# The A12 part of the linear layer by one Strassen level, joined to acc by VectorE, and block sums of x in another order

## Chip, cores and metric

One Trainium2 chip, one of its cores. The metric is the time of the kernel on the device in microseconds (us); the lower the better. Everything is in fp32.

## The reference

```python
# x: (1024, 512); weight: (64, 512, 512); lin_w: (512, 512); lin_b: (512,)
out_lin = x @ lin_w.T + lin_b
xv = einsum('bf,efm->bem', x, weight)
zp = einsum('bf,efm->bem', square(x), square(weight))
y = out_lin + 0.5 * sum(square(xv) - zp, axis=1)
```

The sum over the 64 embeddings e can be drawn into the squared weights for `zp`, so that this needs one matrix product at the end. What remains is 64 products of (1024 x 512) by (512 x 512), their squares summed over e, and one more such product for the linear layer.

## The kernel before

x stands transposed on the chip, with the features on the 128 partitions. It is cut into four blocks A11, A12, A21, A22: r (first digit) is the half of the batch rows, kk (second digit) the half of the features. Each block has four quarters of 256 columns. All products are made by Strassen's algorithm, which gets a 2 by 2 block product from seven products of sums in place of eight; the 64 embeddings' products use two levels of it, so there are 49 products of sums. The outer level (numbers "1" to "7", the code's `i`) combines the blocks of x; the inner level (`o`) combines quarters. `xs` holds all 7 x 7 sums of x, `SLOT` tells where. Of these, "1", "2" and "4" are A11, A12 and A22 as loaded; A21 lies apart. `outer_x(i)` makes the outer sums "5", "6", "7" and "3" (in two parts: three quarters at once, 768 wide, and the fourth, 256 wide), `inner_x(i)` the four inner sums of block i (256 wide). These additions run on VectorE, for "7" and "3" on GpSimd.

The weights are taken four embeddings at a time (16 rounds `q`). GpSimd makes their sums: `outer_t` (L380, 1024 wide), and `inner_t` (L391 `tp`, L393 `t6`, L395 `t4`). A unit (`unit`) is one outer product for one of two column halves j: seven matmuls of 512 columns (L421) into three PSUM tags, x (two banks), v and y (three banks each), with ScalarE copying x to y after the first and VectorE or ScalarE reading the banks between matmuls that accumulate on (L444 to L467). The squares are added to `acc`.

`acc[r]` gathers twice the linear layer and the squares, for the batch half r; `acc_blk(r, b)` is one of its four blocks. The end of the kernel halves it and subtracts half of `zp`.

Before the units the linear layer is put into `acc`. For r = 0, `lin(kk)` multiplies with plain matmuls: eight of 512 columns for A11 (kk = 0) and eight for A12 (kk = 1), four accumulating banks, which `lin_out` (L226) then writes to `acc[0]`, doubled. For r = 1, `lin_p` (L271) does one Strassen level: products "1", "5", "6", "2", "7", "3", "4", each with four matmuls of 256 columns (two kk, two j). Their right-hand sides are the linear weights `lw_sb` or sums of them `LT`, which `lin_t` makes on GpSimd (L284 to L292). Their left-hand sides are quarters of A21 and A22, or sums that `a21_a22_sums` makes (L252): eight additions, seven on VectorE, the eighth, "3" of A22, on GpSimd. Between products, ScalarE copies the bank x to y (L328) or writes twice a bank to `s_lin` or `acc` (`twice`, L303), and VectorE joins twice a bank and a part of `s_lin` into `acc` (`lin_join`, L309).

The order of work is written by hand. `st.at(t, fn)` puts a function at a place t, and `Stream.run` calls them in order of t; the schedule is manual, so each engine executes its instructions in exactly this order, waiting by semaphores for what they need. t is thus a place in a queue and no time. Unit 1 of the first round begins at t = 0. Before it stand, for VectorE: inner sums of "1" (-29) and "2" (-22), the A21/A22 sums (-20), outer and inner "5" (-16), the two joins (-5.5, -3.5), outer and inner "6" (-3.4). For GpSimd: the sums of the linear weights (-30, -29), its one A21/A22 sum, the weight sums of unit 1 (-11.5), of outer "5" (-11), of unit 2 (-5), outer and inner "7" of x (-4.7).

Of the kernel before, what the change touches and what calls it, by code (L numbers as in the profile page):

```python
# [8 lines left out]
F32 = mybir.dt.float32  # L9
AF = mybir.ActivationFunctionType  # L10
ALU = mybir.AluOpType
# [17 lines left out]
def kernel(  # L29
# [31 lines left out]
    nc = tc.nc  # L61
    _, _, _, Q = x.shape
    E, F, M = weight.shape
    P = 128
    NK = F // P
    HM = M // 2
    BK = 2 * HM
# [3 lines left out]
    spool = ctx.enter_context(tc.tile_pool(name="spool", bufs=3))  # L71
    psum = ctx.enter_context(
        tc.tile_pool(name="psum", bufs=3, space=bass.MemoryType.PSUM)
    )
# [19 lines left out]
    def acc_blk(r, b):  # L94
        return acc[r][:, :, b // 2, ts(b % 2, HM)]

    def by_j(bank):
        return bank.rearrange("p (j c) -> p j c", j=2)
# [8 lines left out]
    def xsl(i, o):  # L107
        return xs[:, SLOT[i], SLOT[o], :]

    st = Stream()  # L110
# [5 lines left out]
    lw_sb = T6.rearrange("p u l m -> p (u l) m")  # L116
# [29 lines left out]
    def quarter(r, kk, n):  # L146

        w = slice(0, 3) if n is None else n
        for i, rk in BLOCK.items():
            if rk == (r, kk):  # L150
                return a21[i] if n == 3 else xs[:, SLOT[i], w, :]
        return A21[:, w, :]

    def outer_x(i, eng=nc.vector):
        if i in BLOCK:
            return []

        def put(n):
            w = slice(0, 3) if n is None else n

            def of(o):
                return a21[o] if n == 3 else xs[:, SLOT[o], w, :]

            def src(r, kk):
                return quarter(r, kk, n)

            if i == "5":
                eng.tensor_add(of(i), src(1, 0), src(1, 1))
            elif i == "6":
                eng.tensor_sub(of(i), of("5"), src(0, 0))  # L170
            elif i == "7":
                eng.tensor_sub(of(i), src(0, 0), src(1, 0))
            else:
                eng.tensor_sub(of(i), src(0, 1), of("6"))

        return [lambda: put(None), lambda: put(3)]

    def inner_x(i, eng=nc.vector):
        add, sub = eng.tensor_add, eng.tensor_sub
        return [  # L180
            lambda: add(xsl(i, "5"), a21[i], xsl(i, "4")),
            lambda: sub(xsl(i, "6"), xsl(i, "5"), xsl(i, "1")),
            lambda: sub(xsl(i, "7"), xsl(i, "1"), a21[i]),
            lambda: sub(xsl(i, "3"), xsl(i, "2"), xsl(i, "6")),
        ]
# [7 lines left out]
    LIN = {}  # L193
# [7 lines left out]
            ps = psum.tile([P, BK], F32, tag="y", name=f"y_spin{n}", bufs=3)  # L201
            nc.tensor.matmul(ps, zero[:, 0:P], zero, start=True, stop=True)

    def lin(kk):

        order = [(s, j, l) for s in range(2) for j in range(2) for l in range(2)]
        if kk == 0:
            order.sort(key=lambda o: o[2])
        for s, j, l in order:
            n = 2 * s + j  # L210
            if kk == 0 and l == 0:
                tag = "xxvy"[n]
                LIN[n] = psum.tile(
                    [P, M], F32, tag=tag, name=f"lin{n}", bufs=2 if tag == "x" else 3
                )
            nc.tensor.matmul(  # L216
                LIN[n],
                quarter(0, kk, (0, 1, 3, 2)[2 * s + l])[:, ts(j, P)],
                lw_sb[:, 2 * kk + l, :],
                start=(kk == 0 and l == 0),  # L220
                stop=(kk == 1 and l == 1),
            )

    def lin_out(n):
        s, j = n // 2, n % 2
        nc.scalar.activation(  # L226
            acc[0][:, j, s],
            LIN[n],
            AF.Copy,
            scale=2.0,  # L230
        )

    def lin_x(kk, o):
        if kk == 1:
            return xsl("4", o)
        return A21[:, SLOT[o]] if o in "124" else A21_SUMS[:, "5673".index(o)]
# [3 lines left out]
    def a21_a22_sums():  # L240
        def put(kk, o, eng):
            def of(o):
                return lin_x(kk, o)

            raw = a21["4"] if kk else A21[:, 3]
            fn, a, b = {
                "5": lambda: (eng.tensor_add, raw, of("4")),
                "6": lambda: (eng.tensor_sub, of("5"), of("1")),
                "7": lambda: (eng.tensor_sub, of("1"), raw),
                "3": lambda: (eng.tensor_sub, of("2"), of("6")),  # L250
            }[o]()
            fn(of(o), a, b)  # L252

        return [
            lambda o=o, kk=kk: put(kk, o, nc.gpsimd if o == "3" and kk else nc.vector)
            for o in "5673"
            for kk in range(2)
        ]

    def lin_p(o, bank, first):  # L260
        def fn():
            if o == "1":
                for n in "xvy":
                    LIN[n] = psum.tile(
                        [P, BK], F32, tag=n, name=f"{n}_lin", bufs=2 if n == "x" else 3
                    )
                s_lin = spool.tile([P, 2, BK], F32, tag="s", name="s_lin")
                LIN["s2"], LIN["s5"] = s_lin[:, 0], s_lin[:, 1]
            for kk in range(2):
                for j in range(2):  # L270
                    nc.tensor.matmul(  # L271
                        LIN[bank][:, ts(j, HM)],
                        lin_x(kk, o)[:, ts(j, P)],
                        lin_rhs(lw_sb[:, ts(kk, 2)], LT[kk], o),
                        start=(first and kk == 0 and j == 0),
                        stop=True,
                        skip_group_check=True,
                    )

        return fn  # L280

    def lin_t(t, b):

        nc.gpsimd.tensor_sub(  # L284
            t[:, 0:2, :],
            b[:, :, HM:M],
            b.rearrange("p l m -> p (l m)")[:, 0:M].rearrange(
                "p (u c) -> p u c", u=2
            ),
        )  # L290
        nc.gpsimd.tensor_sub(t[:, 2, :], b[:, 1, HM:M], t[:, 0, :])
        nc.gpsimd.tensor_sub(t[:, 3, :], b[:, 1, 0:HM], t[:, 2, :])  # L292

    def lin_rhs(b, t, o):
        if o in "123":
            l, u = {"1": (0, 0), "2": (1, 0), "3": (1, 1)}[o]
            return b[:, l, ts(u, HM)]
        return t[:, "5764".index(o)]

    def twice(bank, dst):  # L300
        def fn():
            o = by_j(LIN[dst]) if dst in ("s5", "s2") else acc_blk(1, dst)
            nc.scalar.activation(o, by_j(LIN[bank]), AF.Copy, scale=2.0)  # L303

        return fn

    def lin_join(bank, s, blk):
        def fn():
            nc.vector.scalar_tensor_tensor(  # L309
                acc_blk(1, blk),  # L310
                by_j(LIN[bank]),
                2.0,
                by_j(LIN[s]),
                ALU.mult,
                ALU.add,
            )

        return fn

    st.at(-40, spin)  # L320
    for kk in range(2):
        st.at(-30 + 8 * kk, lambda kk=kk: lin(kk))
        st.at(-30 + kk, lambda kk=kk: lin_t(LT[kk], lw_sb[:, ts(kk, 2)]))
    for n in range(4):
        st.at(-20 + 2 * n, lambda n=n: lin_out(n))
    for t, fn in (
        (-14, lin_p("1", "x", True)),
        (-13.5, lambda: nc.scalar.copy(LIN["y"], LIN["x"])),  # L328
        (-12, lin_p("5", "v", True)),
        (-11.5, twice("v", "s5")),  # L330
        (-10, lin_p("6", "y", False)),
        (-9.5, twice("y", "s2")),
        (-8, lin_p("2", "x", False)),
        (-7.5, twice("x", 0)),
        (-6, lin_p("7", "y", False)),
        (-5.5, lin_join("y", "s5", 3)),
        (-4, lin_p("3", "v", False)),
        (-3.5, lin_join("v", "s2", 1)),
        (-2, lin_p("4", "y", False)),
        (-1.5, twice("y", 2)),  # L340
    ):
        st.at(t, fn)

    bias = const.tile([P, M], F32, tag="bias", name="bias")

# [189 lines left out]
    for q in range(NQ):  # L535
# [29 lines left out]
        for k, n, r, times in (  # L565
# [5 lines left out]
            for j in range(2):  # L571
                t = g0 + 14 * k + 7 * j + 14.6
# [11 lines left out]
        st.at(-100, lambda kk=kk, v=v: load_w(0, kk, v))  # L584


    for sums, t in (
        (inner_x("1"), -29),
        (inner_x("2"), -22),
        (a21_a22_sums(), -20),  # L590
        (outer_x("5") + inner_x("5"), -16),
        (outer_x("6") + inner_x("6"), -3.4),
    ):
        for n, fn in enumerate(sums):
            st.at(t + 0.1 * n, fn)
    for i, t in (("7", -4.7), ("3", 36.9)):
        for n, fn in enumerate(outer_x(i, nc.gpsimd) + inner_x(i, nc.gpsimd)):
            st.at(t + 0.1 * n, fn)
# [233 lines left out]
```

## Time and profile before

| | |
|---|---|
| median of 3 runs | 1406.15 us (1405.92 to 1406.15) |
| profiled execution, its own time | 1405.72 us |
| its span (first to last instruction) | 1403.9 us |
| busy: TensorE, VectorE, ScalarE, GpSimd | 1399.7, 869.0, 620.9, 1257.8 us |
| granted TensorE clock | 1.000 |
| linear layer, r = 0, plain matmuls (L216) on the chain | 14.00 us from 4.44 |
| linear layer, r = 1, Strassen products (L271) on the chain | seven of 1.73 us, from 18.44 |
| first matmul of the units (L421) | at 30.36 us |

PE is TensorE, PEld its weight loads, DVE is VectorE, ACT ScalarE, POOL GpSimd, SP SyncE, whose queue issues most loads. A line of a timeline gives the start and the length in us, engine, line of the kernel, operation, output <- inputs by the program's tile names, shape, and in brackets the idle time before it with what released it. The tile name z stands for `ZT`, in which the A21 quarters, their sums and `LT` lie at the start; t stands for `T6`, which first holds `lw_sb`, and for other tiles named t. A fp32 matmul appears as two records, each with its own weight load.

### The profile page before, as it was taken

The numbers are of one execution on the slowest core, as the hardware profiler recorded it, in microseconds if no ns is written. First come the engines' busy times: TensorE is split into PE (matmuls) and PEld (weight loads), VectorE is DVE, ScalarE is ACT, GpSimd is POOL, SyncE is SP. The second block draws the span as 40 slices with busy tenths as digits, with TensorE's granted clock in tenths as the row PEclk, the third lists the DMA queues.
The fourth block names the chain that finished last, engine by engine and source line by source line (L and its number), as shares of the span: only waits on it lengthen the run. The fifth ranks groups of instructions, "written<-read, shape, count | busy, mean of one in ns | idle before, by whom it ended". The sixth has DMA issues, their size and how long they took to land.

```text
span 1403.9 us, 11169 instructions
## 1 busy us (share of the span) xinstructions
PE 1399.7 (100%) x3340; PEld 634.8 (45%) x3340; DVE 869.0 (62%) x1263; ACT 620.9 (44%) x825; POOL 1257.8 (90%) x816
## 2 busy tenths in 40 slices
PE   9999999999999999999999999999999999999999
PEld 5444444444444444444444444444444444444446
DVE  6665656656566665656656566565656656566565
ACT  3444353453535444353453535444353453435443
POOL 7989899998999989898998989989898998989984
PEclk9999999999999999999999999999999999999999
DMA  5299898999989989898999989889898999989975
GB/s 217 60 225 213 192 203 175 221 187 218 197 180 225 182 206 210 192 207 174 222 187 217 202 178 224 179 206 209 199 202 175 225 185 217 202 181 221 181 166 135
DMA packets 58108, 273.63 MB, mean 195 GB/s; under 512 B 5440, under 2 KB 8000, under 8 KB 41792
## 3 DMA queue, kind: packets, MB, share of 16 engines
q0 software_dynamic: 36432, 198.20, 72.0%
q1 hardware_dynamic: 21328, 74.19, 15.1%
q10 hardware_dynamic: 288, 0.52, 0.1%
q8 instruction: 27, 0.44, 0.1%
q14 instruction: 33, 0.27, 0.1%
HBM read 72.61 MB, written 2.10 MB: 53 GB/s over the span
## 4 chain that ended last, share of the span: by engine, by line
PE 99%; DMA 0%; DVE 0%; issue 0%
PE y L421 41%; PE v L421 27%; PE x L421 27%; PE lin L216 1%; PE y_last L659 1%; PE x_last L659 0%; PE v_last L659 0%; PE y_lin L271 0%; DMA t<-lin_wT 0%; PE v_lin L271 0%; PE x_lin L271 0%; PE end L722 0%; DVE z L732 0%
## 5 line engine op out<-in xcount | busy, mean ns | idle before, releaser
L421 PE MATMUL y<-t,xs 128*128 128x512 f32 x896 | 421.3, 592 | 0.0
L475 ACT COPY y<-x 128x512 f32<-128x512 f32 x224 | 127.7, 570 | 610.9 <-PE x L421 610.8
L467 DVE TENSOR_TENSOR z<-y,s 128x512 f32<-128x512 f32 x192 | 132.6, 691 | 242.9 <-PE y L421 242.9
L421 PEld LDWEIGHTS y<-t,xs 128*128 128x128 f32 x896 | 170.1, 190 | 214.2 <-issue 210.4
L497 ACT ACTIVATE z<-z 128x1024 f32<-128x1024 f32 x256 | 260.2, 1054 | 12.0 <-POOL z L472 9.4
L421 PE MATMUL x<-w,xs 128*128 128x512 f32 x512 | 248.4, 592 | 0.0
L421 PE MATMUL v<-tp,xs 128*128 128x512 f32 x448 | 228.8, 592 | 0.0
L421 PE MATMUL y<-tp,xs 128*128 128x512 f32 x448 | 228.8, 592 | 0.0
L506 POOL DMA_DIRECT2D acc<-z x190 | 212.9, 1151 | 15.1 <-DMA acc<-z 11.0
L391 POOL TENSOR_TENSOR tp<-w 128x1024 f32<-128x1024 f32 x64 | 174.9, 2734 | 23.8 <-PE y L421 22.6
L421 PE MATMUL x<-t,xs 128*128 128x512 f32 x384 | 188.3, 592 | 0.0
L472 POOL TENSOR_TENSOR z<-z,s 128x1024 f32<-128x1024 f32 x64 | 149.6, 2354 | 42.7 <-DVE s L467 42.7
L467 DVE TENSOR_TENSOR z<-v,s 128x512 f32<-128x512 f32 x192 | 132.6, 691 | 72.5 <-PE v L421 71.0
L458 DVE TENSOR_TENSOR z<-y,z 128x512 f32<-128x512 f32 x192 | 132.3, 689 | 57.9 <-PE y L421 57.9
L380 POOL TENSOR_TENSOR t<-w,t 128x1024 f32<-128x1024 f32 x64 | 164.2, 2728 | 0.0
L458 DVE TENSOR_TENSOR z<-x,z 128x512 f32<-128x512 f32 x192 | 132.1, 688 | 36.6 <-PE x L421 35.1
L421 PEld LDWEIGHTS x<-w,xs 128*128 128x128 f32 x512 | 97.3, 190 | 122.0 <-issue 121.0
L391 POOL TENSOR_TENSOR tp<-t 128x1024 f32<-128x1024 f32 x48 | 130.0, 2708 | 19.2 <-PE y L421 19.1
L421 PEld LDWEIGHTS v<-tp,xs 128*128 128x128 f32 x448 | 85.1, 190 | 107.1 <-issue 103.1
L421 PEld LDWEIGHTS y<-tp,xs 128*128 128x128 f32 x448 | 85.1, 190 | 106.7 <-issue 106.7
L421 PE MATMUL v<-w,xs 128*128 128x512 f32 x256 | 130.7, 592 | 0.0
L446 DVE TENSOR_TENSOR s<-v,z 128x512 f32<-128x512 f32 x160 | 110.5, 691 | 29.4 <-PE v L421 28.7
(114 smaller groups left out, 1475.7 us busy)
## 6 DMA issues: line engine op xcount, KB each, us to landing
w<-weight SPq DMA_DIRECT2D x64, 1024.0 KB, 13.4
acc<-z POOLq DMA_DIRECT2D x128, 512.0 KB, 8.2
w_sum<-w_sb POOLq DMA_DIRECT2D x63, 1024.0 KB, 9.3
acc<-z POOLq DMA_DIRECT2D x62, 1024.0 KB, 8.1
w<-x SPq DMA_DIRECT2D x2, 1024.0 KB, 8.0
out<-z SPq DMA_DIRECT2D x7, 256.0 KB, 2.3
xs<-x SPq DMA_DIRECT2D x2, 384.0 KB, 7.0
t<-lin_wT ACTq DMA_DIRECT2D x2, 256.0 KB, 4.0
```

The lines of the kernel that those rows point to most:

```text
L216: nc.tensor.matmul(LIN[n], quarter(0, kk, (0, 1, 3, 2)[2 * s + l])[:, ts(j, P)], lw_sb[:, 2 * kk + l, :], start=(kk == 0 and l == 0), stop ...
L380: nc.gpsimd.tensor_sub(OUTER[i][:, u], a[:, u], b[:, u])
L391: nc.gpsimd.tensor_sub(t, b[:, 1], b[:, :, 0])
L421: nc.tensor.matmul(d[bank], xsl(i, o)[:, ts(j, P)], operand_b(q, i, o), start=start, stop=True, skip_group_check=True,)
L446: nc.vector.tensor_add(o, d[bank], zblk(q, addend, j, b))
L458: nc.vector.tensor_add(zblk(q, dst, j, b), d[bank], zblk(q, addend, j, b))
L467: nc.vector.tensor_add(s if both else zblk(q, dst, j, b), d[bank], s)
L472: nc.gpsimd.tensor_add(place(q, n)[:, 1, j], place(q, src)[:, 1, j], d["s"])
L475: st.at(t0 + 0.5, lambda: nc.scalar.copy(d["y"], d["x"]))
L497: lambda u=u: nc.scalar.activation(z[:, u, j], z[:, u, j], AF.Square),
L506: nc.gpsimd.dma_start(o, z, accum_op=ALU.add)
L659: nc.tensor.matmul(ps[:, ts(j, HM)], last_x(i)[:, (0, 1, 3, 2)[2 * s + l], ts(j, P)], last_w(i)[:, l, :], start=(start and j == 0 and l == 0),
```

## The change

- `lin()` has only the eight plain matmuls for A11; `lin_out` follows at once and writes its four banks to `acc[0]`.
- A12 gets the seven Strassen products of `lin_p` with r = 0: two matmuls of 256 columns each, with the inner sums of "2" in `xs` as left-hand sides. ScalarE copies x to y after the first; after each of the six others VectorE executes one scalar_tensor_tensor (`lin_add`), which adds twice the bank to what `acc[0]` or `s_lin` holds. They stand from t = -21.5 to -15.25, one step apart. The second set, r = 1, keeps its places and operations.
- The A21/A22 sums are spread between these, in their old order: -21, -19.5, -18.5, -16.5, -15.5, -15, -14.9 and -14.8.
- Outer "5" and outer "6" of x come together at -14.5, and inner "6" and inner "5" together at -3.4.

```diff
--- before.py
+++ after.py
@@ -201,24 +201,22 @@
             ps = psum.tile([P, BK], F32, tag="y", name=f"y_spin{n}", bufs=3)
             nc.tensor.matmul(ps, zero[:, 0:P], zero, start=True, stop=True)
 
-    def lin(kk):
-
-        order = [(s, j, l) for s in range(2) for j in range(2) for l in range(2)]
-        if kk == 0:
-            order.sort(key=lambda o: o[2])
+    def lin():
+
+        order = [(s, j, l) for l in range(2) for s in range(2) for j in range(2)]
         for s, j, l in order:
             n = 2 * s + j
-            if kk == 0 and l == 0:
+            if l == 0:
                 tag = "xxvy"[n]
                 LIN[n] = psum.tile(
                     [P, M], F32, tag=tag, name=f"lin{n}", bufs=2 if tag == "x" else 3
                 )
             nc.tensor.matmul(
                 LIN[n],
-                quarter(0, kk, (0, 1, 3, 2)[2 * s + l])[:, ts(j, P)],
-                lw_sb[:, 2 * kk + l, :],
-                start=(kk == 0 and l == 0),
-                stop=(kk == 1 and l == 1),
+                quarter(0, 0, (0, 1, 3, 2)[2 * s + l])[:, ts(j, P)],
+                lw_sb[:, l, :],
+                start=(l == 0),
+                stop=(l == 1),
             )
 
     def lin_out(n):
@@ -230,7 +228,9 @@
             scale=2.0,
         )
 
-    def lin_x(kk, o):
+    def lin_x(kk, o, r=1):
+        if r == 0:
+            return xsl("2", o)
         if kk == 1:
             return xsl("4", o)
         return A21[:, SLOT[o]] if o in "124" else A21_SUMS[:, "5673".index(o)]
@@ -257,22 +257,23 @@
             for kk in range(2)
         ]
 
-    def lin_p(o, bank, first):
+    def lin_p(r, o, bank, first):
         def fn():
             if o == "1":
                 for n in "xvy":
-                    LIN[n] = psum.tile(
-                        [P, BK], F32, tag=n, name=f"{n}_lin", bufs=2 if n == "x" else 3
+                    LIN[r, n] = psum.tile(
+                        [P, BK], F32, tag=n, name=f"{n}_lin{r}", bufs=2 if n == "x" else 3
                     )
-                s_lin = spool.tile([P, 2, BK], F32, tag="s", name="s_lin")
-                LIN["s2"], LIN["s5"] = s_lin[:, 0], s_lin[:, 1]
-            for kk in range(2):
+                s_lin = spool.tile([P, 2, BK], F32, tag="s", name=f"s_lin{r}")
+                LIN[r, "s2"], LIN[r, "s5"] = s_lin[:, 0], s_lin[:, 1]
+            kks = range(2) if r else (1,)
+            for kk in kks:
                 for j in range(2):
                     nc.tensor.matmul(
-                        LIN[bank][:, ts(j, HM)],
-                        lin_x(kk, o)[:, ts(j, P)],
+                        LIN[r, bank][:, ts(j, HM)],
+                        lin_x(kk, o, r)[:, ts(j, P)],
                         lin_rhs(lw_sb[:, ts(kk, 2)], LT[kk], o),
-                        start=(first and kk == 0 and j == 0),
+                        start=(first and kk == kks[0] and j == 0),
                         stop=True,
                         skip_group_check=True,
                     )
@@ -299,47 +300,48 @@
 
     def twice(bank, dst):
         def fn():
-            o = by_j(LIN[dst]) if dst in ("s5", "s2") else acc_blk(1, dst)
-            nc.scalar.activation(o, by_j(LIN[bank]), AF.Copy, scale=2.0)
+            o = acc_blk(1, dst) if isinstance(dst, int) else by_j(LIN[1, dst])
+            nc.scalar.activation(o, by_j(LIN[1, bank]), AF.Copy, scale=2.0)
 
         return fn
 
-    def lin_join(bank, s, blk):
+    def lin_add(r, bank, addend, dst):
+
+
+        def of(n):
+            return acc_blk(r, n) if isinstance(n, int) else by_j(LIN[r, n])
+
         def fn():
             nc.vector.scalar_tensor_tensor(
-                acc_blk(1, blk),
-                by_j(LIN[bank]),
-                2.0,
-                by_j(LIN[s]),
-                ALU.mult,
-                ALU.add,
+                of(dst), by_j(LIN[r, bank]), 2.0, of(addend), ALU.mult, ALU.add
             )
 
         return fn
 
     st.at(-40, spin)
+    st.at(-30, lin)
     for kk in range(2):
-        st.at(-30 + 8 * kk, lambda kk=kk: lin(kk))
         st.at(-30 + kk, lambda kk=kk: lin_t(LT[kk], lw_sb[:, ts(kk, 2)]))
     for n in range(4):
-        st.at(-20 + 2 * n, lambda n=n: lin_out(n))
-    for t, fn in (
-        (-14, lin_p("1", "x", True)),
-        (-13.5, lambda: nc.scalar.copy(LIN["y"], LIN["x"])),
-        (-12, lin_p("5", "v", True)),
-        (-11.5, twice("v", "s5")),
-        (-10, lin_p("6", "y", False)),
-        (-9.5, twice("y", "s2")),
-        (-8, lin_p("2", "x", False)),
-        (-7.5, twice("x", 0)),
-        (-6, lin_p("7", "y", False)),
-        (-5.5, lin_join("y", "s5", 3)),
-        (-4, lin_p("3", "v", False)),
-        (-3.5, lin_join("v", "s2", 1)),
-        (-2, lin_p("4", "y", False)),
-        (-1.5, twice("y", 2)),
-    ):
-        st.at(t, fn)
+        st.at(-29 + 0.1 * n, lambda n=n: lin_out(n))
+    for r, t0, dt in ((0, -21.5, 1), (1, -14, 2)):
+
+        def copy_y(r=r):
+            nc.scalar.copy(LIN[r, "y"], LIN[r, "x"])
+
+        for n, (o, bank, first, fn) in enumerate(
+            (
+                ("1", "x", True, copy_y),
+                ("5", "v", True, twice("v", "s5") if r else lin_add(0, "v", 3, "s5")),
+                ("6", "y", False, twice("y", "s2") if r else lin_add(0, "y", 1, "s2")),
+                ("2", "x", False, twice("x", 0) if r else lin_add(0, "x", 0, 0)),
+                ("7", "y", False, lin_add(r, "y", "s5", 3)),
+                ("3", "v", False, lin_add(r, "v", "s2", 1)),
+                ("4", "y", False, twice("y", 2) if r else lin_add(0, "y", 2, 2)),
+            )
+        ):
+            st.at(t0 + dt * n, lin_p(r, o, bank, first))
+            st.at(t0 + dt * n + 0.25 * dt, fn)
 
     bias = const.tile([P, M], F32, tag="bias", name="bias")
 
@@ -584,15 +586,16 @@
         st.at(-100, lambda kk=kk, v=v: load_w(0, kk, v))
 
 
-    for sums, t in (
+    for sums, *times in (
         (inner_x("1"), -29),
         (inner_x("2"), -22),
-        (a21_a22_sums(), -20),
-        (outer_x("5") + inner_x("5"), -16),
-        (outer_x("6") + inner_x("6"), -3.4),
+        (a21_a22_sums(), -21, -19.5, -18.5, -16.5, -15.5, -15),
+        (outer_x("5") + outer_x("6"), -14.5),
+        (inner_x("6") + inner_x("5"), -3.4),
     ):
         for n, fn in enumerate(sums):
-            st.at(t + 0.1 * n, fn)
+            k = min(n, len(times) - 1)
+            st.at(times[k] + 0.1 * (n - k), fn)
     for i, t in (("7", -4.7), ("3", 36.9)):
         for n, fn in enumerate(outer_x(i, nc.gpsimd) + inner_x(i, nc.gpsimd)):
             st.at(t + 0.1 * n, fn)
```

## The prediction

> **What bounds the kernel now.** I read the page's first and fourth parts, then the chain of waits, then the timelines of TensorE (PE), VectorE (DVE), ScalarE (ACT) and GpSimd (POOL) over the first 45 us, the only place that the change touches. From the page, busy time by engine and shares of the chain:
>
> ```profile
> PE 1399.7 (100%) x3340; PEld 634.8 (45%) x3340; DVE 869.0 (62%) x1263; ACT 620.9 (44%) x825; POOL 1257.8 (90%) x816
> PE 99%; DMA 0%; DVE 0%; issue 0%
> ```
>
> PE carries 99% of the chain: a matmul fewer is gained one for one, a PE wait is lost one for one, and no slack elsewhere can give it back. From the chain in order of time (start, length):
>
> ```profile
> 4.44 14.00 PE lin L216 x32
> 18.44 1.73 PE x_lin L271 x8
> ...
> 28.80 1.73 PE y_lin L271 x8
> ```
>
> PE runs without a gap from 4.44. Matmul records come two to a matmul, so 32 records are 16 matmuls of the linear layer's upper half; then seven Strassen products of four 256-wide matmuls each, 1.73 us a product.
>
> Now the engines beside it, DVE first (start, length, tile, idle before):
>
> ```profile
> 12.66 0.41 DVE L252 TENSOR_TENSOR z<-z 128x256 f32<-128x256 f32 x1
> ...
> 17.19 2.47 DVE L182 TENSOR_TENSOR xs<-xs 128x256 f32<-128x256 f32 x1
> 19.58 1.48 DVE L183 TENSOR_TENSOR xs<-xs,z 128x256 f32<-128x256 f32 x1
> 20.99 1.49 DVE L184 TENSOR_TENSOR xs<-xs 128x256 f32<-128x256 f32 x1
> 27.19 0.69 DVE L309 SCALAR_TENSOR_TENSOR acc<-y_lin,s_lin 128x512 f32<-128x512 f32 x1 [4.72 <-PE y_lin L271]
> ```
> ```profile
> 14.16 2.72 POOL L252 TENSOR_TENSOR xs<-xs 128x256 f32<-128x256 f32 x1 [2.37 <-DVE xs L252]
> 16.84 2.54 POOL L391 TENSOR_TENSOR tp<-w 128x1024 f32<-128x1024 f32 x1
> 19.45 1.33 POOL L393 TENSOR_TENSOR t<-w,tp 128x512 f32<-128x512 f32 x1
> 20.86 1.33 POOL L395 TENSOR_TENSOR t<-w,t 128x512 f32<-128x512 f32 x1
> 22.15 4.85 POOL L380 TENSOR_TENSOR t<-w,w 128x1024 f32<-128x1024 f32 x2
> ```
>
> The same 256-wide block sum takes 0.41 us while POOL is idle and 1.48 to 2.47 us while POOL computes. The ends show why: POOL's L391 ends at 19.38 and DVE's L182 0.28 later; POOL's L393 ends at 20.78 and DVE's L183 0.28 later; L395 at 22.19 and L184 at 22.48. Each DVE sum sits out one whole POOL instruction, and POOL's next one, issued first, goes ahead of DVE's next. They alternate one for one. Before, this cost nothing: DVE was done at 22.48 and then idle 4.72 us until the first join at 27.19.
>
> **What the skill says.** The Trainium skill, "SBUF — State Buffer", section "Who interferes with whom", says that a VectorE instruction with two SBUF inputs contends with a GpSimd instruction that reads SBUF and the second to issue fully blocks, while one with at most one SBUF input doesn't contend. The trace agrees: the 2.47 us above, against 0.69 us for the join (one PSUM input) at 27.19, inside POOL's L391 of 26.96 to 29.31. "PSUM — Partial Sum Buffer", section "PSUM bank collisions raise a hardware error", wants PSUM guarded by semaphore per bank: a matmul into bank y waits until the reader of y is through. The trace shows one such hand-over with one product between: ACT's copy runs 31.42 to 31.99, and the next matmul but one starts at 33.07 instead of 32.94, 0.13 us late. "TensorE: Matmul & The Clock Gate", section "Part 1: The HAM clock gate", says that an idle window of about 3.4 us halves the PE clock. Here the spin matmuls at the start are 0.85 us apart per pass, later passes 0.43: agreed for a cold start; no idle stretch inside this run tests the rest.
>
> **The change, part by part.**
>
> 1. *Matmuls.* Eight of the 16 512-wide matmuls go: 8 x 0.858 = 6.87 us (in the PE timeline 21 matmuls from 39.11 to 57.14 take 18.03). Fourteen 256-wide ones come: 14 x 0.432 = 6.05 (28 take 12.09 from 18.27 to 30.36). Gain **0.82 us**. The order of the first eight and the DMA loads are unchanged, so they start at 4.44 as now.
>
> 2. *PSUM hand-overs in the new seven products*, which are 0.865 us apart where the old seven are 1.73. P1 would start at 11.41, P5 at 12.27. P6 needs ACT's copy of x to y, with one product between: 0.13 as in the first unit. P7 needs y after DVE has read it for s2, P4 needs y after DVE has read it for block 3, again one product between, and DVE's read is 0.69 against ACT's 0.57: 0.13 + 0.12, about 0.24 each. Sum **+0.61 us** (0.3 to 1.2). The four `lin_out` activations (0.60 each) are done by 12.2, ahead of their readers.
>
> 3. *DVE's new order.* Inner sums of x for "2" end at 12.7 as now. Then come, interleaved, the A21/A22 sums and seven joins of 0.69 that wait for PE (the old kernel had two). So sum 6 of A22, over at 14.08 now, runs behind the join of P7: P7 ends 16.10, join 16.30 to 16.99, sum at about 17.3. POOL's own sum (L252) waits for it and stands first in POOL's queue, ahead of the weight sums of unit 1: POOL starts them at 18.1 instead of 16.84, 1.3 us late. That alone costs nothing: their first use, unit 1's P5, is at 31.22.
>
> 4. *What is now behind what.* After sum 6, DVE still has seven two-SBUF sums before the second set's joins: A21's 7, A22's 7, A21's 3, outer 5 in two parts, outer 6 in two parts; outer 6 stood behind those joins until now. From 18.1 POOL has work without a gap. With holds from the rows above (POOL 2.23 for 1024 wide, 17.15 to 19.38; 1.12 for 512; DVE 0.28 for 256 wide, 0.81 for 768 wide, 30.66 to 31.47):
>  - A21's 7 behind L252: to 18.40.
>  - A22's 7 behind tp (18.40 to 20.63): to 20.91. The join of P4 goes in the gap.
>  - A21's 3 behind t6 (to 22.03): 22.31.
>  - outer 5 behind t4 (to 23.43): 24.24; its second part behind L380 (to 26.47): 26.75.
>  - outer 6 behind the second L380 (to 28.98): 29.79; its second part behind the tp of unit 2 (to 32.02): 32.30.
>
>  Then, and only then, the join of bank y of the second set: 32.24 to 32.93. P7 of that set is over at 26.71, and P4 accumulates onto the same bank. P4's turn is 28.44; with the hand-over (0.22) it starts at 33.15. **Stall 4.71 us.** Queued behind the join are the second join and the inner sums; behind P4 on PE is everything.
>
> 5. *The stretch after.* Inner 6 and inner 5, eight sums, replace outer 6 and inner 6, six sums (29.44 to 37.43 now). Alternating with POOL's t6, t4 and x7 sums they end at about 41.5. The units then begin at 34.88 and want their first join of y by about 41.8: no stall, and the 0.1 us that PE now loses at 38.15 goes. POOL's later weight sums are 2.6 us later, PE 4.5: their cover grows.
>
> ACT, SP and all DMAs keep their order; their work lies far from these waits, so I cost it at nothing.
>
> Sum: -0.82 + 0.61 + 4.71 - 0.1 = **+4.4 us**. The profiled execution has span 1403.9 and own time 1405.72; with 4.4, 1410.1. The median shown is 0.43 above that execution, so **1410.5**. A measurement of this kernel can tell about 0.2%, 2.8 us, from no change. The new order's stall is in no row of before. Its bounds: 0, if DVE gets through between POOL instructions; 4 to 5.2, if POOL's start moves by half a microsecond; and, as PE is idle over 3.4 us, a halved clock after it, which by the page's 3.4 us window and one or two such windows at half speed is an estimate of 1.7 to 3.4 more. I take no drop, because the window must fall within a gap only 1.3 us longer, and keep it for the range.
>
> **Rivals.**
> - *Clock drop* (0.24): the stall and 1.7 to 3.4 us more, up to 1413.9.
> - *DVE goes first* (0.18), the case on the other side: not slower. One row speaks for it: POOL's L252 at 14.16 takes 2.72 us, while DVE ran five sums back to back at full speed; POOL got in only when DVE paused at 16.3. If DVE's run of sums shuts POOL out so, outer 6 is done before 26.9 and P4 doesn't wait. Then only the eight inner sums from 29.2 count: nine microseconds of alternation to 38.3, the y join of unit 1 wanted by 36.6, a stall of 1.7 at most. Sum -0.82 + 0.61 + 1.6: 1407.5 (1406.3 to 1408). It decides if two of the four POOL instructions after 22.3 fall behind DVE. Against it: at 7.99, 19.58 and 35.62 a ready DVE sum stood behind POOL each time.
> - *All hidden* (0.11): just parts 1 and 2, 1405.3 to 1406.3; the same would be seen if the half of the layer didn't go to Strassen's form at all.
>
> **How the numbers follow.** Stall without clock drop 0.44, with it 0.24: slower 0.68. DVE first 0.18 and hidden 0.11 are within 0.2%: with a little rounding 0.29. Faster by 2.8 us needs more than the change removes from PE plus all of its waits now: 0.03. Range 1406.5 to 1413.6: it takes in the rival that isn't slower, and leaves out the hidden case, faster, and the top of the clock drop. The likeliest's own range is 1409.9 to 1411.2.
>
> **What would show it.** Right: 14 matmuls of 256 between 11.4 and about 18; POOL's L252 near 17.4; a PE gap of about 4.7 us before the second set's P4, released by DVE, whose outer 6 sums (L170) end next to 32 at 2 us or more each. Wrong: L170 done before 27, or DVE sums of 0.41 us after 18. PE passes 0.85 apart after the gap would show the clock drop; waits of over 0.5 us inside the first set, that part 2 is too small.

## The result and the profile after

The changed kernel takes **1413.26 us** (median of 6 runs, 1412.26 to 1414.0) against 1406.16 before (6 runs): ratio 1.005, 95% interval 1.0039 to 1.0061, 7.1 us slower. The profiled execution has 1413.42 us of its own and span 1411.6. First the page's busy times:

```profile
PE 1403.0 (99%) x3352; PEld 640.5 (45%) x3352; DVE 879.9 (62%) x1269; ACT 621.4 (44%) x826; POOL 1257.2 (89%) x816
```

Then the chain of waits in order of time (start, length), which had been PE alone from 4.44 on:

```profile
4.71 7.17 PE lin L214 x16
...
24.53 2.50 DVE z L168
27.03 0.18 DVE xs L170
27.21 2.77 issue
29.99 2.55 DVE z L170
32.54 0.61 DVE acc L315
33.15 0.04 issue
33.20 3.78 PE y_lin L272 x8
36.98 1.71 PE x L423 x2
```

The 16 plain matmuls are 8 (16 records), but now VectorE's block sums carry the chain from 17 to 33 us, and P4 (product "4") of the second set, r = 1, begins at 33.20. A product of that set takes 1.73 us elsewhere; this one takes 3.78 on the chain. PE's timeline at the start of the first set, at the start of the second and around that P4:

```profile
11.72 1.03 PE L272 MATMUL x_lin<-t,xs 128*128 128x256 f32 x4
...
18.35 1.03 PE L272 MATMUL x_lin<-t,z 128*128 128x256 f32 x4
...
27.85 1.03 PE L272 MATMUL v_lin<-t,xs 128*128 128x256 f32 x4
33.20 2.08 PE L272 MATMUL y_lin<-z,z 128*128 128x256 f32 x4 [4.32 <-DVE acc L315]
35.06 1.92 PE L272 MATMUL y_lin<-z,xs 128*128 128x256 f32 x4
36.77 1.91 PE L423 MATMUL x<-w,xs 128*128 128x512 f32 x2
```

From start to start, two kk halves of a product are 0.86 us apart, so P4 was due at 28.71, and it takes 3.57 us to the next product. VectorE's and GpSimd's timelines (start, length, operation, idle before):

```profile
19.21 1.97 DVE L252 TENSOR_TENSOR xs<-xs,z 128x256 f32<-128x256 f32 x1
21.10 1.49 DVE L252 TENSOR_TENSOR z<-z 128x256 f32<-128x256 f32 x1
22.51 2.02 DVE L168 TENSOR_TENSOR xs<-z,xs 128x768 f32<-128x768 f32 x1
24.46 2.58 DVE L168 TENSOR_TENSOR z<-z 128x256 f32<-128x256 f32 x1
26.96 3.10 DVE L170 TENSOR_TENSOR xs<-xs 128x768 f32<-128x768 f32 x1
29.99 2.55 DVE L170 TENSOR_TENSOR z<-z 128x256 f32<-128x256 f32 x1
32.47 0.68 DVE L315 SCALAR_TENSOR_TENSOR acc<-y_lin,s_lin 128x512 f32<-128x512 f32 x1
```
```profile
17.68 0.73 POOL L252 TENSOR_TENSOR xs<-xs 128x256 f32<-128x256 f32 x1 [5.67 <-DVE xs L252]
18.36 2.53 POOL L393 TENSOR_TENSOR tp<-w 128x1024 f32<-128x1024 f32 x1
20.97 1.34 POOL L395 TENSOR_TENSOR t<-w,tp 128x512 f32<-128x512 f32 x1
22.39 1.33 POOL L397 TENSOR_TENSOR t<-w,t 128x512 f32<-128x512 f32 x1
23.68 3.07 POOL L382 TENSOR_TENSOR t<-w,w 128x1024 f32<-128x1024 f32 x1
26.72 2.53 POOL L382 TENSOR_TENSOR t<-w,w 128x1024 f32<-128x1024 f32 x1
29.21 3.05 POOL L393 TENSOR_TENSOR tp<-w 128x1024 f32<-128x1024 f32 x1
```

Six sums in a row each end 0.3 us (256 wide) or 0.8 us (768 wide) after a GpSimd instruction: L393 ends at 20.89, the sum beside it at 21.18. Only after the sixth comes the join at 32.47, though P7, whose bank it reads, was done at 26.98. Last, PE's busy time and granted clock (the third number from the end) from P4's start to unit 1's second set of x matmuls, after and before:

```profile
33.20:40.43 7.23, 7.23 (x14) 4.42 (x15) 7.16 (x8) 1.75 (x3) 6.99 (x7) 0.60 0.00 0
```
```profile
28.64:33.07 4.43, 4.43 (x15) 2.58 (x14) 4.20 (x4) 1.75 (x3) 4.27 (x4) 1.00 0.00 0
```

The same matmuls take 7.23 us in place of 4.43, at a clock of 0.60: the gap cost its length and 2.80 us more. Finer stretches of the changed kernel show when the clock fell:

```profile
28.71:32.12 3.41, 0.16 (x1) 0.00 (x0) 3.41 (x2) 0.00 (x0) 3.41 (x2) 1.00 0.00 0
32.12:33.20 1.08, 0.01 (x1) 0.01 (x1) 1.08 (x3) 0.00 (x0) 1.00 (x2) 0.50 0.00 0
33.20:38.95 5.75, 5.75 (x11) 3.86 (x12) 5.71 (x6) 0.83 (x2) 5.51 (x6) 0.50 0.00 0
```

It was at half for 6.83 us. The first 1.08 us of them lie in the gap, where nothing runs; 5.75 lie on matmuls, and half of that, 2.9, is an estimate of the loss that agrees with the 2.80.

The profiled difference of 7.7 us adds up so: the second set starts at 18.35 instead of 18.27, although the first load landed 0.27 later; gap 4.49; slow passes 2.80; and some 0.3 at the end, where a last gather landed after 10.7 us instead of 9.7, which the prediction doesn't have.

### The profile page after: what moved, and what is told of

Same layout as the page of the kernel before. It is cut to its first block, busy times and chain, and to the rows that moved or that the text cites. A ratio compares the mean times of both kernels' runs of the same rounds, so it can differ in the third digit from the quotient of the medians.

```text
span 1411.6 us, 11203 instructions
## 1 busy us (share of the span) xinstructions
PE 1403.0 (99%) x3352; PEld 640.5 (45%) x3352; DVE 879.9 (62%) x1269; ACT 621.4 (44%) x826; POOL 1257.2 (89%) x816
## 4 chain that ended last, share of the span: by engine, by line
PE 95%; POOL 2%; DVE 1%; DMA 1%; issue 1%; POOLq 0%; ACTq 0%; ACT 0%; DVEq 0%
PE y L423 40%; PE x L423 27%; PE v L423 27%; DMA acc<-z 1%; PE lin L214 1%; PE y_lin L272 0%; POOL z L474 0%; POOL acc L508 0%; DMA t<-lin_wT 0%; POOL w_sb L652 0%; DVE z L170 0%; DVE z L168 0%; POOL tp L393 0%; POOL w L632 0%; POOL t L636 0%
## 5 line engine op out<-in xcount | busy, mean ns | idle before, releaser
L393 POOL TENSOR_TENSOR tp<-w 128x1024 f32<-128x1024 f32 x64 | 175.6, 2744 | 23.8 <-PE y L423 22.5
L393 POOL TENSOR_TENSOR tp<-t 128x1024 f32<-128x1024 f32 x48 | 130.0, 2708 | 18.9 <-PE y L423 18.8
```

What stands on the lines that cost most here:

```text
L393: nc.gpsimd.tensor_sub(t, b[:, 1], b[:, :, 0])
```

## The experiments

All edits are to the changed kernel unless said otherwise. The median of before moves by up to 0.5 us from one series of runs to another (1406.03 to 1406.49), so differences are taken to the one beside each.

**Order of the sums alone** (an edit of the kernel before):

```diff
-        (outer_x("5") + inner_x("5"), -16),
-        (outer_x("6") + inner_x("6"), -3.4),
+        (outer_x("5") + outer_x("6"), -16),
+        (inner_x("6") + inner_x("5"), -3.4),
```

> The kernel before with only the order of the x sums changed: outer 5 and outer 6 early, inner 6 and inner 5 late; A12 stays with plain matmuls. Theory (two-SBUF sums of VectorE alternate one for one with GpSimd, and what counts is how many stand ahead of the next join): outer 6 is done by about 20, the two joins are on time, no gap before P4 and no clock drop; then eight sums from 29.4 end at about 38.5 instead of 37.4, so unit 1's join of y comes some 1.1 us late: +0.8 to +1.4 us on before, 1407.3. Rival (the new order of the sums is by itself what costs): a large part of the 7 us, over +3.

Measured: 1407.2 (13 runs) against 1406.25; ratio 1.0008, interval 0.9999 to 1.0016. The profile has one new PE wait in unit 1, of 0.87 us. So the new order by itself costs some 0.95 us by the medians, about what the theory says, though the interval just includes no change. One detail didn't go as expected. VectorE and then GpSimd in this kernel:

```profile
14.91 0.42 DVE L252 TENSOR_TENSOR z<-z 128x256 f32<-128x256 f32 x1
15.25 0.95 DVE L168 TENSOR_TENSOR xs<-z,xs 128x768 f32<-128x768 f32 x1
16.12 0.42 DVE L168 TENSOR_TENSOR z<-z 128x256 f32<-128x256 f32 x1
16.45 0.95 DVE L170 TENSOR_TENSOR xs<-xs 128x768 f32<-128x768 f32 x1
17.32 0.42 DVE L170 TENSOR_TENSOR z<-z 128x256 f32<-128x256 f32 x1
```
```profile
14.40 3.92 POOL L252 TENSOR_TENSOR xs<-xs 128x256 f32<-128x256 f32 x1 [2.37 <-DVE xs L252]
```

Here VectorE was already in a run of sums when GpSimd's came, and GpSimd sat out all of them: 3.92 us for an addition that takes 0.73 alone. Outer 6 was through at 17.7, at full speed. The same two outer sums, placed behind GpSimd's start in the changed kernel, took until 32.5.

**The old groups of sums:**

```diff
-        (outer_x("5") + outer_x("6"), -14.5),
-        (inner_x("6") + inner_x("5"), -3.4),
+        (outer_x("5") + inner_x("5"), -14.5),
+        (outer_x("6") + inner_x("6"), -3.4),
```

> The changed kernel with the old groups of x sums: outer 5 + inner 5 ahead of the joins of the second set, outer 6 + inner 6 behind. Theory: eight instead of six sums wait behind GpSimd ahead of the join, the last ones behind t6, t4 and a 768-wide sum; join of y at about 34.8 instead of 32.5, gap about 2.4 us longer (near 6.8 us): +2.5 us on the changed kernel, 1415.7. Rival (the join is late from VectorE's own work; uncontended, four inner sums of 0.34 are as long as outer 6's 1.2): the same as the changed kernel within 0.3 us.

Measured: 1415.04 (4 runs) against 1406.25, 8.8 us over before and 1.7 more than the changed kernel's own 7.1. PE's timeline shows the gap:

```profile
35.40 2.08 PE L272 MATMUL y_lin<-z,z 128*128 128x256 f32 x4 [6.58 <-DVE acc L315]
```

It is 6.58 us, and the same line of the changed kernel says 4.32: 2.3 us more, with 2.4 expected, from two additional short sums. VectorE's own work can't give that; what counts is how many GpSimd instructions the sums stand behind. The time grew by less than the gap because the slow passes took 1.5 us here (the stretch of 4.43 us took 5.92) where they took 2.80 there. The clock says why:

```profile
28.65:31.40 2.75, 0.17 (x1) 0.00 (x0) 2.71 (x2) 0.00 (x0) 2.75 (x2) 1.00 0.00 0
31.40:35.40 4.00, 0.00 (x0) 0.00 (x0) 4.00 (x5) 0.00 (x0) 3.84 (x4) 0.50 0.00 0
35.40:38.24 2.84, 2.84 (x7) 2.31 (x8) 2.81 (x4) 0.00 (x0) 2.76 (x3) 0.50 0.00 0
```

It fell 2.75 us into the gap and was at half for the same 6.8 us, but 4.00 of them passed while TensorE stood still. A longer gap took up more of the slow time.

**TensorE kept busy in the gap, by five matmuls of zeros, then by two:**

```diff
+    def fill():
+        zero = nc.const_aps.tensor(0.0, [P, BK], F32)
+        ps = psum.tile([P, BK], F32, tag="y", name="y_fill", bufs=3)
+        for n in range(5):  # or 2
+            nc.tensor.matmul(ps, zero[:, 0:P], zero, start=True, stop=True)
+
+    st.at(-2.1, fill)
```

> The changed kernel with five matmuls of zeros (0.86 us each, 4.3 us in all) put into TensorE's gap ahead of the second set's P4; nothing waits for their result. Theory (the gap halves the clock after it): P4 starts at 33.2 as without them, at full speed, and the 2.8 us of slow passes go: 1410.5. Rival (the slow passes after the gap come from something else, such as waits on weights or banks): 1413.2 as the changed kernel, or longer.

> As with five, but two matmuls of zeros (1.7 us), which run right after P3 and leave TensorE idle for about 2.7 us. Theory with the skill's window of 3.4 us: an idle stretch shorter than the window does not drop the clock: 1410.5. Rival (the clock drops on any such stall, or on low activity within a window): some or all of the 2.8 us stay, 1411.5 to 1413.3.

> A repeat of the changed kernel with five matmuls of zeros in TensorE's gap, in more rounds, beside the other kernel of this call. Theory (the clock drop is the only effect of the gap beyond its length): 5.0 +- 0.4 us above before and 2.2 to 2.8 below the changed kernel. Rival (the first result, 1411.1, hides a cost of the filling itself): over 5.5 above before.

Five: 1411.14 (5 runs) against 1406.25, and in the repeat, which also has five, 1410.76 (6 runs) against 1406.49; ratios 1.0033 (1.002 to 1.0045) and 1.0031 (1.002 to 1.0043). That is 4.9 and 4.3 us over before instead of 7.1; the second lies just below the 4.6 to 5.4 expected. PE's timeline with five:

```profile
28.54 4.47 PE L325 MATMUL y_fill<-const-float32-0.0 128*128 128x512 f32 x10
33.02 1.13 PE L272 MATMUL y_lin<-z,z 128*128 128x256 f32 x4
33.99 1.03 PE L272 MATMUL y_lin<-z,xs 128*128 128x256 f32 x4
```

P4 starts when it did without them and takes 1.83 us instead of 3.57. So the join is as late as ever; what went is the slow clock, which the records give as 1.000 in every one of these runs, and as 0.997 to 0.999 in all six of the changed kernel. By the medians 2.2 to 2.8 us of the loss are the clock, the rest the wait.

With two the four runs fall apart: 1410.45 and 1410.49 at a clock of 1.000, 1412.85 and 1413.46 at 0.999. The gap was 2.6 us in the profile (one of the runs at 1.000). So such a gap slows the clock in some executions and not in others. The theory that needs a gap of 3.4 us fails; of the two rivals, any stall fails too, and low activity within a window is left, without a threshold.

**Outer 6 moved back behind the joins:**

```diff
-        (outer_x("5") + outer_x("6"), -14.5),
-        (inner_x("6") + inner_x("5"), -3.4),
+        (outer_x("5"), -14.5),
+        (outer_x("6") + inner_x("6") + inner_x("5"), -3.4),
```

> The changed kernel with outer 6 alone moved back behind the second set's joins (ahead of inner 6 and inner 5). Theory: the join of y is free at about 27.1, P4 starts on time (gap under 0.3 us); but ten sums now stand ahead of unit 1's first join and end at about 43.5 where 36.9 is wanted: the gap moves into unit 1, 5 to 7 us, with slow passes after it: 1412 to 1416. Rival (only the place of outer 6 ahead of the linear joins costs): 1405.9 to 1407.

Measured: 1414.41 (4 runs) against 1406.03. P4 of the second set is on time, and PE's timeline has the gap in unit 1:

```profile
38.25 1.02 PE L423 MATMUL y<-t,xs 128*128 128x512 f32 x2
45.52 2.05 PE L423 MATMUL y<-t,xs 128*128 128x512 f32 x2 [6.24 <-DVE z L469]
47.36 3.58 PE L423 MATMUL x<-w,xs 128*128 128x512 f32 x4
```

Ten sums now stand ahead of unit 1's join. The wait isn't tied to the linear layer: whichever join comes behind the contended sums is late.

**The sums given to GpSimd, and then the two sets interleaved.** Besides the edit, GpSimd's sum 3 of A22 goes to -14.1. The second kernel has also `((0, -21.5, 2), (1, -16.5, 2))` as the sets' places.

```diff
-        (outer_x("5") + outer_x("6"), -14.5),
-        (inner_x("6") + inner_x("5"), -3.4),
+        (outer_x("5"), -14.5),
+        (outer_x("6", nc.gpsimd), -14.4),
+        (inner_x("6", nc.gpsimd), -4.7),
+        (inner_x("5", nc.gpsimd), 37.5),
...
-    for i, t in (("7", -4.7), ("3", 36.9)):
+    for i, t in (("7", 21), ("3", 36.9)):
```

> The changed kernel with outer 6, inner 6 and inner 5 of x computed by GpSimd, GpSimd's sum 3 of A22 behind outer 6, and outer and inner 7 later in GpSimd's queue. VectorE's last sums are then done before GpSimd computes. Theory: no sum of VectorE waits for GpSimd after about 21, all joins on time, no gap, no clock drop; what is left is 0.82 us of matmuls gained against 0.58 of hand-overs: 1405.6 to 1406.1. Rival (GpSimd with eight more sums becomes late for the units' weights): a gap in units 2, 6 or 7, over 1407.

> As with the sums on GpSimd, and the products of the two linear sets interleaved, so that another set's product lies between a bank's matmul, its reader and the next matmul into it. Theory: most of the 0.58 us of hand-overs goes: 0.4 to 0.5 us less, 1405.2 to 1405.6. Rival (the hand-overs are no waits but a cost of every product into y): as with the sums on GpSimd, within 0.1.

Measured: 1416.86 and 1414.82 (5 runs each) against 1406.03. The half that I was after came out: VectorE's joins were on time, PE had no gap up to 74 us. But the rival was right on the whole. GpSimd, which waited for VectorE until 20.9 us and then had ten more sums (the expectation says eight), was late with unit 7's weight sum t4. PE's waits of the first and the second kernel:

```profile
PE y L423 <- ACT s L446: 3.0, 1, 3.0
PE y L423 <- POOL t L397: 2.0, 1, 2.0
```
```profile
PE y L423 <- ACT s L446: 5.5, 1, 5.5
PE y L423 <- POOL t L397: 1.1, 1, 1.1
```

The longer gap comes later, and the first kernel's chain leads it back to the same late t4 (L397), behind which GpSimd issued a gather of squared weights:

```profile
76.16 10.89 DMA w_sum<-w_sb
```

It landed at 87.05; ScalarE's next squares waited for it, and behind them stood the copies that PE needed. The clock fell again, at the shorter gap too:

```profile
76.55 1.98 PE L423 MATMUL y<-t,xs 128*128 128x512 f32 x2 [1.97 <-POOL t L397]
76.55:80.92 4.37, 4.37 (x6) 1.83 (x7) 1.35 (x2) 0.00 (x0) 4.29 (x3) 0.61 0.97 193
```

The times can't show the hand-overs, but the timelines do: from the first product to unit 1 the 42 matmuls of the two sets took 18.72 us in the first kernel and 18.21 in the second, where 42 of 0.432 make 18.14. Interleaving took away 0.5 us of waits, as expected.

**The joins in VectorE's old gap.** Both sets stay in Strassen's form. They are interleaved so that VectorE's queue up to 22.5 us can be that of before, and the eight joins follow where VectorE had been idle; outer 6 stands behind them, and inner 6 goes to GpSimd. The places are PE's products (`PT`) and the joins and copies (`FT`):

```diff
-    for r, t0, dt in ((0, -21.5, 1), (1, -14, 2)):
+    PT = (
+        (-21.5, -21, -19.5, -18, -16.5, -16, -15),
+        (-20.5, -20, -19, -18.5, -17.5, -17, -15.5),
+    )
+    FT = (
+        (-21.4, -17.9, -17.8, -17.7, -16.3, -15.8, -14.8),
+        (-20.4, -19.9, -18.9, -18.4, -17.2, -16.8, -15.4),
+    )
+    for r in range(2):
...
-        (a21_a22_sums(), -21, -19.5, -18.5, -16.5, -15.5, -15),
-        (outer_x("5") + outer_x("6"), -14.5),
-        (inner_x("6") + inner_x("5"), -3.4),
+        (a21_a22_sums(), -21.6),
+        (outer_x("5") + inner_x("5"), -20.8),
+        (outer_x("6"), -3.4),
+        (inner_x("6", nc.gpsimd), 0.1),
```

> Both linear sets by Strassen's form as in the changed kernel, but with the two sets' products interleaved, the A21/A22 sums, outer 5 and inner 5 of x all ahead of the joins (VectorE's queue up to 22.5 us as in the kernel before), the eight joins in the stretch in which VectorE was idle before, outer 6 after them on VectorE and inner 6 on GpSimd. Theory (the loss is only sums queued ahead of joins while GpSimd computes, and GpSimd started late): GpSimd starts its weight sums at 16.8 as before, no join waits, no gap, no clock drop, and the 0.82 us of matmuls are gained, less up to 0.3 of hand-overs: 1405.2 to 1405.8 with before at 1406.2. Rival (six more joins on VectorE can't be hidden ahead of unit 1): gaps of over 0.5 us before P3, P4 or in unit 1, 1406.5 or more.

Measured: 1406.52 (13 runs) against 1406.49; ratio 1.0001, interval 0.9992 to 1.0009. The 7 us are gone with both sets still in Strassen's form: no gap in the linear layer, whose 42 matmuls took 18.13 us. It differs from the changed kernel in several places at once, so the runs don't say which of them suffices. The 0.82 us of gain did not show: the time, and a gap of over 0.5 us in unit 1, are what the rival forecast. But the wait there was not for a join (PE's waits; 0.2 us more came at the end of the kernel):

```profile
PE y L431 <- ACT y L485: 0.6, 1, 0.6
```

ScalarE's squares of the first weights (1.99 us) now stood between the last copy of the linear layer and unit 1's copy. The last kernel puts them ahead:

```diff
-            w_times = (-6, 14.8, 37, 56.6)
+            w_times = (-16.9, 14.8, 37, 56.6)
```

> As the kernel with the joins in the gap, with ScalarE's first two squares of weights (1.99 us) placed ahead of the second set's last copy instead of behind it. Theory (in that kernel the copy of unit 1 stood behind the squares and TensorE waited 0.72 us for it): that wait goes, so 0.4 to 0.8 us less than with the joins in the gap and 0.3 to 0.8 below before: 1405.7 with before at 1406.3. Rival (the squares wait for weights there and push the copies of the linear sets): no gain, 1406.5 or more.

Measured: 1405.96 (13 runs) against 1406.22; ratio 0.9997, interval 0.9989 to 1.0006. Both waits are gone from the profile. That is 0.26 below its before, where the kernel without this edit was 0.03 above: in the expected direction, just short of the expected 0.3 to 0.8, and not told apart from before.

## Why the prediction was right

**Sign and range held; the middle was 2.8 us low.** 1413.26 lies within 1406.5 to 1413.6, near the top, and outside the likeliest case's own range of 1409.9 to 1411.2. It is the case called clock drop, which I gave 0.24. That it fell inside is in part luck: the range left out the top of that case, and one of the six executions, 1414.0, lies above it.

1. *Matmuls*: eight go, fourteen of 256 columns come, as predicted. With the next term it comes to -0.19 us (the second set 0.08 later after a start 0.27 later), predicted -0.21.
2. *Hand-overs*: the first set took 6.63 us (11.72 to 18.35) where fourteen matmuls without waits take 6.05: 0.58, predicted 0.61. By the starts in PE's timeline ScalarE's hand-over cost 0.08 us and VectorE's two 0.26 and 0.24, where 0.13 and 0.24 each were predicted. (In the row of before the matmul that waited for ScalarE's copy is the one at 32.13; by 33.07 the 0.13 us are lost, so the size was read rightly.)
3. *GpSimd's late start*: its sum of A22 at 17.68, predicted 17.4; `tp` at 18.36, predicted 18.1.
4. *The alternation*: outer 6 over at 32.54, predicted 32.30; P4 at 33.20, predicted 33.15; gap 4.49, predicted 4.71. Each of the seven sums ends 0.2 to 0.3 us later than forecast, about as much as the first load was late; the gap is shorter because P4 came 0.05 us after the join and not 0.22. The old-groups kernel and the one with outer 6 moved back show that this is the cause: the gap lengthens with the number of sums behind GpSimd and moves with their place.
5. *The stretch after*: the eight sums ended at 41.74, predicted 41.5, and unit 1's first join still waited for PE (1.46 us). No wait, as predicted, though here the slow passes gave the sums 2.8 us more. The kernel with five filling matmuls, at full clock, is the fair test: its sums ended at 41.58, and PE had no wait there either. The 0.1 us that was to go at 38.15 is 0.03 in the rows of before (two matmuls from 37.36 to 39.11).

**The step that was off** is the term for the clock, taken as zero. I argued that a whole 3.4 us window would have to fall inside the gap. The runs showed otherwise. In the changed kernel's profile the clock did fall 3.41 us into the gap, but all six executions had a clock below 1, in the old-groups kernel it fell after 2.75 us, a gap of 2.6 us did it in two runs of four, and in the kernel with the sums on GpSimd a gap of 1.97 us did (three matmuls of 0.86 us took 4.37). What low activity suffices I did not measure. The size, 2.80 us in the profile, lies in the 1.7 to 3.4 that I estimated from the Trainium skill ("TensorE: Matmul & The Clock Gate", section "Part 1: The HAM clock gate"); with the filling matmuls it was 2.2 to 2.8 by the medians. Had I put both branches at even chances, nothing in the profile of before would have been against it.

**The rival that VectorE goes first** was wrong for the changed kernel and right about the row it stood on. The kernel with the order alone shows the behaviour in full: a run of sums without a pause keeps GpSimd out until it ends, 3.92 us. In the changed kernel joins stand between the sums, GpSimd gets in once beside one of them (17.68), and from then on its next instruction is ahead of VectorE's next. That the joins let it in is read from the timelines; no run changed that alone. I had left the two rows side by side; the condition between them, who is in a run when the other comes, is by these timelines what the change altered. Why GpSimd's request at 14.40 didn't go ahead of sums that VectorE issued later, as it does in the alternation, stays open.

## What to carry to other kernels

An instruction that waits for TensorE, put into a queue of cheap independent ones, can cost more than its own time: it delays what another engine needs first, and as the timelines read, it lets that engine in between. Before a VectorE sum is moved, count the GpSimd instructions that it will stand behind and what waits behind it; the same outer sums were over at 17.7 us in one place and 32.5 in another. Where TensorE is the bound, price a gap at its length and the slow passes after it; the slow time that runs out within the gap costs nothing.

## What the runs showed of the hardware

- A TensorE gap of 0.87 or 1.10 us left the clock at 1.00; 1.97 us lowered it in the one profile that has it; 2.6 us did so in two runs of four; the gap of 4.3 us in all six. In the changed kernel and the old-groups kernel the clock was at half for 6.8 us, from 3.41 and 2.75 us into the gap; the slow passes after a gap cost 1.5 to 2.8 us.
- TensorE fed with zeros keeps its clock: five matmuls of zeros left it at 1.000 in all 11 runs and took 2.2 to 2.8 us off the whole.
- Between VectorE sums with two SBUF inputs and GpSimd sums there are two regimes: one for one, and GpSimd shut out for a whole run (3.92 us for an addition of 0.73).
